# Regrouping layer 1's contractions on one Trainium2 core: two jobs of two per image, with free places ahead of them and behind the projections

## The chip, the cores and the metric

The kernel runs on one core of a Trainium2 chip. That core has a tensor engine (PE in the profile, with PEld for its loads of weights), a vector engine (DVE), a scalar engine (ACT), a GpSimd engine (POOL) and a sync engine (SP), which here does nothing but issue transfers. Each engine works through its own instructions in order and waits on semaphores for the others. Transfers run on 16 DMA engines. The metric is the time of one execution on the device, in microseconds (us); the time of before is the median of three runs.

## The reference: what is computed

The input `x` is 8 images of 56 x 56 pixels with 384 channels, in float32. Two layers of "outlook" attention follow each other, each around a group normalisation and with a residual sum. Cut to layer 1, the one that the change touches:

```python
x = x + conv1(group_norm(x, G=32))          # layer 0 has the same frame around its own conv0

def conv1(x):                               # HEADS = 6, K = 3, head width 64
    a = softmax((x @ W_attn + b_attn).reshape(B, H*W, 6, 9))   # nine weights a pixel and head
    v = x @ W_v + b_v
    patches = stack([pad(v)[:, i:i+H, j:j+W] for i in range(3) for j in range(3)])
    y = einsum('bpKhd,bphK->bphd', patches, a)                 # weighted sum of the 3x3 neighbours
    return y @ W_proj + b_proj
```

Each pixel gets, per head, nine weights from a softmax, takes the weighted sum of the values of its 3x3 neighbours, and is projected. Layer 0 is richer (nine outputs per pixel, which are folded back), and its code is not changed.

## The kernel before

The images are taken in four pairs; a pair's 112 rows lie on the partitions, and the kernel walks over the 56 columns of each pair. Seven columns make a block (`PX = 7`), so each pair has eight blocks and layer 1 has 32, numbered `g`. One step of layer 1's loop (line 1290) is one column.

For each column `attend` (line 1105) projects 128 pixels to the 54 weights and 384 values: three matmuls into one of three PSUM tiles called `bank` (f32 matmuls stand as two records each in the trace, so six). Since 112 rows don't fill 128 partitions, eight columns are packed into seven tiles, and in one step of eight `attend` does nothing ("the attend falls out"). DVE adds the biases; POOL stores the weights into the tile of the block (`at`, kept in `xr_home` and `xin_home`) and the values into a table in DRAM, `vtab`.

When a block's columns are complete, `weigh` and `share` do its softmax on DVE and ACT, and `move` (line 1157) shifts it between rows with three matmuls (`pw` in the trace) and copies it with nine ACT copies into `wz`, which SP sends to one of three tables in DRAM, `ztab`. From there SP loads the block's weights as a banded matrix: `z`, two transfers for each image (`bands`). The values come back as patches, `vp`, one transfer for each image (`fetch_v`): image 0's at step `turn == 5` and image 1's inside `fetch` (line 1195). `z` has three buffers, `vp` has two.

`fetch` then queues the block's jobs on PE. `contract(t)` multiplies a patch row tile: 12 matmuls, 90 rows by 64 columns of the array, into a PSUM tile `pc` of which there are two (`NC = 2`); ACT copies it to `yT`. Each image has four of them, t = 0 to 3, the last of half size: 24, 24, 24 and 12 records. When both images are in `yT`, `project_out(half, j)` (line 1230) does six projections (`po`): three channel groups for the first four columns of the block, three for the other three. DVE adds bias and residual and transposes the result into `ot`; after the third of each half four transfers `out<-ot` are put on the list `later`, which `flush` sends out on SP's queue.

The order of all this is written out by hand. `Jobs` (line 359) is a list of jobs with due steps, and each step of the loop gives it two places: one ahead of `attend` (line 1301) and one behind `attend` and `move` (line 1324). A place takes one job, if the first in the list is due. Seven steps have 14 places. A block's list has seven jobs of contractions (image 0: t = 0 and 1 together, then 2, then 3; image 1: four single ones), one empty job, and six projections: 14. Behind each of the two places stands a `flush`; `fetch`, with its loads of `z` and of image 1's `vp`, stands at the end of the step with `turn == 0`. SP's queue therefore has its transfers in the order in which the loop wrote them.

In the profile all matmuls stand under line 129 and all other operations of layer 1 under line 144, since helpers record them; they are told apart by their tiles. `wv_t` is the home of layer 1's output weights in `po<-yT,wv_t`.

Of the kernel before, what the change touches and what calls it, by code (L numbers as in the profile page):

```python
# [15 lines left out]
def two_outlook_layers(  # L16
# [89 lines left out]
    def by_quadrant(ap, r0, col, n, b):  # L106
        first = r0 * W * C + col * C + b * QC
        return bass.AP(ap.tensor, ap.offset + first, [[W * C, R], [C, n], [1, QC]])
# [19 lines left out]
    def matmul(*args, **kwargs):  # L128
        tc.keep_in_program_order(nc.tensor.matmul(*args, **kwargs))  # L129
# [26 lines left out]
    def projected(name):  # L156
        return patch.tile([P, NCH, PX, IMG, H], F32, tag="yT", name=f"yT_{name}", bufs=1)
# [187 lines left out]
    def bands(queue, z, table, line, slot, row, top, groups, b, py, npy):  # L345

        for (s0, s1), (m0, m1) in groups:
            first = (b * H + top) * line + s0 * slot + m0 * row
            queue.dma_start(
                z[s0:s1, :, m0 * row : m1 * row],  # L350
                bass.AP(
                    table.tensor, table.offset + first + bands.at[row],
                    [[slot, s1 - s0], [py * line, npy], [1, (m1 - m0) * row]],
                ),
            )
# [34 lines left out]
    jobs, norms = Jobs(), Jobs()  # L390
# [26 lines left out]
    def project_half(po, w, yT, half, j):  # L417
        lo, hi = HALVES[half]
        for i in range(NCH):
            matmul(  # L420
                po[:, : (hi - lo) * R],
                w[:, i, j * P : (j + 1) * P],
                yT[:, i, lo:hi].rearrange("p m b y -> p (m b y)"),
                start=(i == 0), stop=(i == NCH - 1),
            )

    def layer0(late, pools):
# [508 lines left out]
        normed(1, SHARED, both=True)  # L936
        LAG = 4
        ahead = layer1((xr_home, xt_homes, xin_home, xn_homes, wa_home, wv_t), late_w)
        last_step = NPAIR * W - 1
        first_of = {last_step - 40: 1, last_step - 7: 1, last_step - 6: 1, last_step - 5: 1}  # L940
# [98 lines left out]
    def layer1(homes, late_w):  # L1039
# [19 lines left out]
        def load(g, queue=sync):  # L1059
            pair, px = divmod(g, NPX)  # L1060

            if g % 5 == 4:
                t = wide(3, lambda size: late_w.tile(size, F32, tag="xres", name="wide_3", bufs=1))
            elif g % 5 == 3:
                t = halves[3]
            elif g % 5 == 2:
                t = wide(2, lambda size: pool.io.tile(size, F32, name="wide_2", bufs=1))
            else:
                t = wide(g % 5, lambda size: (xr_home, wa_home)[g % 5][:, : size[1]])
            t = t[:, : NCH * T].rearrange("p (i t) -> p i t", i=NCH)  # L1070
            queue.dma_start(t, x1s[pair][px])
            x1ts[g] = t.rearrange("p i (m r) -> p i m r", m=PX)
# [117 lines left out]
        def fetch_v(g, b):  # L1190

            vps[g, b] = patch_tiles(f"1_{g}", b)[: SX1 * SY1, :NPY1]
            rows_to_patches(sync, vps[g, b], vtab1, g % NPX, b * H + MARGIN - 1, PY1, NPY1, SX1)

        def fetch(g, due):
            pair, px = divmod(g, NPX)
            n_tile = 2
            yT = projected(f"1_{g}")
            x1t = x1ts.pop(g)
            for b in range(IMG):  # L1200
                bands(
                    sync, zs1[(g * IMG + b) % NZ], ztab1[g % NTAB1], LINE1, SLOT1, ROW1, MARGIN - 1,
                    GROUPS1, b, PY1, NPY1,
                )
            fetch_v(g, 1)
            for b in range(IMG):
                z, vp = zs1[(g * IMG + b) % NZ], vps.pop((g, b))

                def contract(t, b=b, z=z, vp=vp):
                    lo, hi = t * n_tile, min(NPY1, (t + 1) * n_tile)  # L1210
                    pc = ps.tile([P, NCH, n_tile, PY1, PX], F32, tag="c", name=f"pc1_{g}_{b}_{t}", bufs=NC)
                    for py in range(lo, hi):
                        zp = z[:, py].rearrange("s (y h m) -> s y h m", y=PY1, h=HEADS1)
                        for h in range(HEADS1):
                            i, j = divmod(h, P // D1)
                            matmul(
                                pc[j * D1 : (j + 1) * D1, i, py - lo],
                                vp[:, py, h * D1 : (h + 1) * D1],
                                zp[:, :, h, :],
                                start=True, stop=True,  # L1220
                            )
                    scalar.copy(
                        yT[:, :, :, b, lo * PY1 : hi * PY1],
                        pc[:, :, : hi - lo].rearrange("p i n y m -> p i m (n y)"),
                    )

                for ts in ((0, 1), (2,), (3,)) if b == 0 else ((0,), (1,), (2,), (3,)):
                    jobs.add(due, lambda ts=ts, f=contract: [f(t) for t in ts])

            def project_out(half, j):  # L1230
                lo, hi = HALVES[half]
                n = (hi - lo) * R
                po = ps.tile([P, 4 * R], F32, tag="ot"[(half + j) % 2], name=f"po1_{g}_{half}_{j}")
                project_half(po, wo_t, yT, half, j)
                res = x1t[:, j, lo:hi].rearrange("p m r -> p (m r)")
                vector.scalar_tensor_tensor(
                    res, po[:, :n], bo_t[:, j : j + 1], res, ALU.add, ALU.add
                )

                if j == 0:  # L1240
                    fetch.ot = pool.io.tile([P, NR * 4 * QC], F32, tag="ot", name=f"ot_{g}_{half}")
                ot = fetch.ot[:, : NR * (hi - lo) * QC]
                vector.transpose(
                    ot.rearrange("p (s m c) -> p s m c", s=NR, c=QC)[:, :, :, j::NCH],
                    bass.AP(
                        x1t.tensor, x1t.offset + j * T + lo * R,
                        [x1t.ap[0], [1, NR], [R, hi - lo], [NR, Q]],
                    ),
                )
                if j == NCH - 1:  # L1250
                    for b in range(NQ):
                        later.append(
                            lambda b=b: sync.dma_start(
                                by_quadrant(out, pair * R, px * PX + lo, hi - lo, b),
                                ot[b * Q : b * Q + LANES],
                            )
                        )

            if g:
                jobs.add(due, lambda: None)  # L1260
            for half in range(2):
                for j in range(NCH):
                    jobs.add(due, lambda half=half, j=j: project_out(half, j))

        load(0, nc.gpsimd)
        rows_of_channels(wc_t[:, :, :NA1], wa1, nc.gpsimd)
# [23 lines left out]
        for step in range(AHEAD, (NG + 1) * PX + BEHIND):  # L1290
# [41 lines left out]
            if of > 1 and turn == 0:  # L1332
                assert len(cleared) >= min(2 * of - 2, NZ)
                fetch(of - 2, base + step + 3)
            if of == NG and turn == 4:
                fetch_v(NG - 1, 0)
                fetch(NG - 1, base + step + 1)
            elif 0 < of < NG and turn == 5:
                fetch_v(of - 1, 0)
# [49 lines left out]
```

## Time and profile before

| | us |
|---|---|
| three runs | 3172.67, 3184.32, 3172.41 (median 3172.67) |
| the profiled execution | 3169.09 |
| its span | 3166.6, mean granted clock of PE 0.991 |
| layer 1 in full swing, 2300 to 2500: PE busy | 199.55 of 200 |
| the same stretch, DVE / ACT / POOL busy | 100.47 / 48.04 / 80.91 |
| the same stretch, DMA share and rate | 0.96, 237 GB/s |
| start of the first contraction of neighbouring blocks | 2448.88, 2480.99, 2513.10 |

The profile gives each engine's busy time, groups of instructions by line and tile, and a chain of waits: from the last instruction back to what released it, step by step. A line of the chain has its start, its length and what it was, with the number of records. SPq lines are transfers issued by SP: their length is the time that the issuing took, not that of the transfer. "DMA share" is the mean busy share of the 16 DMA engines. Bracketed at the end of a line of the timeline is the idle time ahead of it and what ended it. The layers overlap for a while around 2100 us, where layer 0 ends.

### The profile page before, as it was taken

What the parts mean: (1) busy time and instruction counts of PE and PEld (TensorE: products, weight loads), DVE (VectorE), ACT (ScalarE), POOL (GpSimd) and SP (SyncE); (2) the same over time, 40 slices, a digit from 0 to 9 for tenths busy, and PEclk for the clock granted to TensorE, in tenths of its full rate; (3) what the DMA queues carried; (4) which work ended last, traced back from release to release, by engine and by line L of the source; (5) the groups of instructions that cost most, each with busy time, mean ns of one, the idle gap of its engine ahead of it and who ended that gap; (6) DMA issues with size and microseconds to landing.
All of it is one profiled execution on the core that took longest, in us unless ns stands there. A gap on an engine that the chain in (4) does not pass through costs nothing. (4 is left out here: it accounts for less than half of the span.)

```text
span 3166.6 us, 72796 instructions
## 1 busy us (share of the span) xinstructions
PE 3065.6 (97%) x27640; PEld 2093.9 (66%) x27640; DVE 2079.1 (66%) x4945; ACT 1007.4 (32%) x2426; POOL 1645.7 (52%) x2758
## 2 busy tenths in 40 slices
PE   6899999999999999999999999989999999999998
PEld 5667766777777777776676677645656666565655
DVE  5777777777777777777777677735545454545545
ACT  4333343333333333333333233322222222222221
POOL 2765566565556665666566566643443434344440
PEclk9999999999999999999999999999999999999999
DMA  9799987899998799998889897898999999999997
GB/s 298 223 302 316 321 262 259 297 311 297 311 311 268 255 299 299 318 293 289 274 275 257 291 309 239 259 347 213 231 234 238 240 232 237 237 230 236 234 237 169
DMA packets 619841, 850.84 MB, mean 269 GB/s; under 512 B 264927, under 2 KB 496563, under 8 KB 611171
## 3 DMA queue, kind: packets, MB, share of 16 engines
q1 hardware_dynamic: 554946, 726.37, 76.8%
q0 software_dynamic: 63968, 118.11, 12.3%
q8 instruction: 217, 3.56, 0.5%
q10 hardware_dynamic: 576, 1.72, 0.2%
q14 instruction: 134, 1.09, 0.1%
HBM read 514.86 MB, written 322.17 MB: 264 GB/s over the span
## 5 line engine op out<-in xcount | busy, mean ns | idle before, releaser
L129 PE MATMUL bank<-wa_t,xn 128*128 128x288 f32 x3528 | 971.6, 412 | 16.3 <-ACT xn L144 9.8
L144 POOL TENSOR_TENSOR at<-at,d 128x972 f32<-128x972 f32 x196 | 441.3, 2251 | 713.9 <-DVE d L144 389.0
L129 PEld LDWEIGHTS bank<-wa_t,xn 128*128 128x128 f32 x3528 | 649.9, 191 | 227.4 <-issue 17.6
L144 ACT ACTIVATE at<-at 128x972 f32<-128x972 f32 x196 | 198.7, 1014 | 950.5 <-DVE at L144 950.2
L144 DVE TENSOR_REDUCE mx<-bank 128x36 f32<-128x324 f32 x588 | 284.3, 483 | 315.3 <-PE bank L129 313.5
L129 PE MATMUL bank<-xt,xn 128*128 128x438 f32 x1176 | 477.6, 542 | 2.8 <-ACT xn L144 2.8
L129 PE MATMUL po<-yT,wo_t 128*128 128x336 f32 (+1 forms) x1152 | 417.6, 499 | 15.4 <-DVE x1t L144 14.9
L129 PE MATMUL bank<-wv_t,xn 128*128 128x384 f32 x1176 | 415.7, 490 | 0.0
L129 PEld LDWEIGHTS pc<-z,vp 121*32 121x32 f32 (+1 forms) x17664 | 335.7, 118 | 112.0 <-issue 83.2
L129 PE MATMUL po<-yT,wv_t 128*128 128x336 f32 (+1 forms) x1152 | 394.1, 494 | 2.5 <-ACT yT L144 2.5
L129 PE MATMUL pc<-z,vp 121*32 121x49 f32 (+1 forms) x17664 | 373.2, 217 | 17.1 <-issue 8.6
L144 ACT COPY yT<-pc 128x294 f32<-128x294 f32 (+2 forms) x512 | 206.0, 411 | 428.2 <-PE pc L129 425.2
L129 PEld LDWEIGHTS po<-yT,wv_t 128*128 128x128 f32 x1152 | 218.8, 190 | 170.9 <-issue 123.0
L129 PEld LDWEIGHTS bank<-xt,xn 128*128 128x128 f32 x1176 | 214.5, 190 | 171.9 <-issue 151.8
L129 PEld LDWEIGHTS po<-yT,wo_t 128*128 128x128 f32 x1152 | 214.8, 192 | 147.2 <-issue 75.5
L144 DVE TENSOR_TENSOR at<-bank,mx 128x324 f32<-128x324 f32 x588 | 291.3, 495 | 31.0
L129 PEld LDWEIGHTS bank<-wv_t,xn 128*128 128x128 f32 x1176 | 221.6, 191 | 132.8 <-issue 10.4
L144 POOL DMA_DIRECT2D vtab<-v x476 | 289.4, 612 | 15.3 <-DMA vtab<-zeros 6.4
L144 POOL TENSOR_TENSOR pre<-at,at 112x108 f32<-112x108 f32 (+1 forms) x440 | 236.6, 538 | 76.9 <-DMA at<-at 29.1
L144 DVE TENSOR_TENSOR xt<-bank,ba_t 128x54 f32<-128x54 f32 x147 | 31.1, 212 | 262.9 <-PE bank L129 252.9
L144 ACT ACTIVATE wts<-pre,inside 112x48 f32<-112x48 f32 (+4 forms) x672 | 179.3, 358 | 74.3 <-DMA ztab<-wts 62.6
L1123 POOL DMA_DIRECT2D xin_home<-xt x147 | 76.8, 526 | 212.7 <-DVE xt L144 196.0
(136 smaller groups left out, 3279.9 us busy)
## 6 DMA issues: line engine op xcount, KB each, us to landing
z<-ztab SPq DMA_DIRECT2D x64, 2352.0 KB
vp<-vtab SPq DMA_DIRECT2D x64, 1536.0 KB
vp<-vtab SPq DMA_DIRECT2D x64, 945.0 KB
xres<-xT SPq DMA_DIRECT2D x32, 1176.0 KB
ztab<-wts SPq DMA_DIRECT2D x336, 110.2 KB
xin_home<-xT SPq DMA_DIRECT2D x52, 672.0 KB
xr_home<-in_x SPq DMA_DIRECT2D x50, 672.0 KB
vtab<-v POOLq DMA_DIRECT2D x100, 336.0 KB, 6.7
```

The source lines that it names most:

```text
L129: tc.keep_in_program_order(nc.tensor.matmul(*args, **kwargs))
L144: return lambda *args, **kwargs: tc.keep_in_program_order(op(*args, **kwargs))
L1123: nc.gpsimd.dma_start(at_of(g_of)[row : row + n, m_of].rearrange("r k h -> r (k h)"), lg[lo : lo + n])
```

## The change

Image 0's contractions become two jobs, t = 0 and 1, then t = 2 and 3; image 1's as well. One empty job stands ahead of image 0's first, and two empty jobs stand behind the last projection. The empty job between contractions and projections stays. A block's list is then 1 + 2 + 2 + 1 + 6 + 2 = 14 long, as before.

```diff
-                for ts in ((0, 1), (2,), (3,)) if b == 0 else ((0,), (1,), (2,), (3,)):
+                if b == 0:
+                    jobs.add(due, lambda: None)
+                for ts in ((0, 1), (2, 3)):
                     jobs.add(due, lambda ts=ts, f=contract: [f(t) for t in ts])
...
             for half in range(2):
                 for j in range(NCH):
                     jobs.add(due, lambda half=half, j=j: project_out(half, j))
+            for _ in range(2):
+                jobs.add(due, lambda: None)
```

The orders that result for a block in which no attend falls out, in PE's program order (c0.1 is image 0, t = 1; A an attend; w the move's matmuls; P0 to P5 the projections):

```
before  c0.0 c0.1 c0.2 A w c0.3 c1.0 A c1.1 c1.2 A c1.3 A P0 P1 A P2 P3 A P4 P5 A
after   c0.0 c0.1 A w c0.2 c0.3 c1.0 c1.1 A c1.2 c1.3 A P0 P1 A P2 P3 A P4 P5 A A
```

and of SP's queue, in a block that also loads `x` (the residual of a later block):

```
before  ztab  x  vp(image 0)  z x4  vp(image 1)  out x4  out x4
after   ztab  x  vp(image 0)  out x4  z x4  vp(image 1)  out x4
```

Engines' instructions are the same in number and kind. POOL's order is the same.

## The prediction

> **What bounds the kernel now.** I read the page first, then the busy time by stage, then the chain that ended last inside layer 1, then SP's timeline there.
>
> ```profile
> PE 3065.6 (97%) x27640; PEld 2093.9 (66%) x27640; DVE 2079.1 (66%) x4945; ACT 1007.4 (32%) x2426; POOL 1645.7 (52%) x2758
> ```
>
> ```profile
> 2481.00:2513.00 32.00, 32.00 (x246) 19.35 (x246) 15.50 (x30) 8.24 (x24) 12.77 (x24) 1.00 1.01 253
> ```
>
> The second is one 32 us block of seven columns of layer 1 (columns: length; PE, PEld, DVE, ACT, POOL busy; granted clock; DMA share; GB/s). Two things are full at once: PE has no idle time, and the DMA share is 1.01. The chain of the same block:
>
> ```profile
> 2480.99 2.35 PE pc L129 x72
> 2483.34 2.40 PE bank L129 x6
> 2485.74 0.66 PE pw L129 x6
> 2486.40 1.19 PE pc L129 x36
> 2487.59 2.40 PE bank L129 x6
> 2489.99 1.54 PE pc L129 x48
> 2491.54 2.40 PE bank L129 x6
> 2493.94 0.49 PE pc L129 x12
> 2494.43 2.40 PE bank L129 x6
> 2496.84 4.51 PE po L129 x12
> 2501.35 2.21 PE bank L129 x6
> ```
>
> Four runs of contractions (pc), with an attend (bank) between them, then the six projections (po; the last four, with an attend falling out among them, run from 2503.55 to 2510.89). An attend takes 2.40 us behind a pc run and 2.21 behind po: 0.19 us is the change of weights. Runs of 12, 36 and 48 records take 0.49, 1.19 and 1.54 us, so a run costs 0.14 us plus 29.2 ns a record. SP's queue beside it:
>
> ```profile
> 2487.45 0.31 SPq L144 DMA_DIRECT2D ztab<-wz  x1
> 2487.82 0.57 SPq L144 DMA_DIRECT2D wide<-x  x1
> 2488.61 2.15 SPq L144 DMA_DIRECT2D vp<-vtab  x1
> 2493.97 4.61 SPq L144 DMA_DIRECT2D z<-ztab  x4
> 2498.69 0.49 SPq L144 DMA_DIRECT2D vp<-vtab  x1
> 2507.70 7.75 SPq L144 DMA_DIRECT2D out<-ot  x5
> ```
>
> With S the start of a block's first contraction (2480.99), the next block's z are issued at S+13.0, the second vp at S+17.7, the output of the first half (out0) at S+26.7. The next block contracts from S+32.1. So z and vp have 14 to 19 us to land, and what SP waits for longest, the transposed output, comes behind them.
>
> **The change part by part.** The empty places emit nothing: cost 0 by themselves. What they do is shift jobs by whole places against the attends and against the DMA issues.
>
> *PE.* A block's runs become 48 (image 0, first two), attend, pw, 84 (image 0, last two, and image 1, first two), attend, 36. One run fewer saves 0.14+0.19 = 0.33 us. The 72 run of before had 0.11 us of waiting in it (2.35 against 0.14+72x29.2 ns), which goes. New: in the 84 run the third contraction needs the PSUM buffer of the first, whose ACT copy stands behind the nine wz copies. The trace has that run in the blocks where an attend falls out:
>
> ```profile
> 2357.20 0.67 PE pw L129 x6
> ...
> 2359.10 1.61 PE pc L129 x48
> ```
>
> From pw's end, 2357.87, to the run's end, 2360.71: 2.84 us instead of 2.59. Its first copy was the short one (0.30 us); now it is one of 0.44, so 2.95. Per block: 1.54+2.95+1.19 = 5.68 against 5.57, less 0.19 for one attend: -0.1 us. Bounds: -0.44 (no wait) to +0.2. In the 4 blocks where the attend ahead of pw falls out, the two norm activations of 1.79 us stand ahead of those copies as well: some +1.4 each, between 0 and 1.8. Sum over 29 blocks: -3+6, about nothing. POOL's order is unchanged; DVE and ACT get the same work; DVE is half idle (15.5 of 32 us).
>
> *SP.* This is what decides. The projections come two places earlier: the third (the last of the first half) is now ahead of the block's z loads in program order. So SP's order becomes out0 (4 DMAs), z (4), vp, out1 (4), ztab, x, vp, where it was z, vp, out0, out1, ztab, x, vp. SP issues in order, and out0 waits for DVE's transposes. Behind it now wait z and the second vp of the next block, and out1, ztab, x and vp behind those; for z and vp waits PE. Call T0 the moment out0 is issued.
>
> From the start of image 1's contractions (in the 84 run) to T0: two contractions 1.54, attend 2.40, run of 36 1.19, attend 2.40, two projections 4.51, attend 2.21, third projection 2.24 (half of two); then DVE's add 0.68 and transpose 1.11 and 0.06 of gaps. 16.5+1.85 = 18.35 us.
>
> From T0 to image 1's contractions of the next block: out0's four issues of 0.82 to 0.87 us in the last blocks, then z's first packet 0.8 us behind its issue: 4.4 to 5.4, I take 5.0. The packets of z (840 bytes) and of vp (1536 bytes) are seen in the trace: at the very end, with no stores of POOL beside them, z and vp took 9.9 us (3132.3 to 3142.2); in a full block 14.3 (2468.5 to 2482.8, with up to 1.5 us of neighbours in it). Three attends' stores still fall in the new place, fewer than in a full block since PE will wait: I take 12.6, nearer to the full block. Landing: 1.1 to 1.3 us from the last packet to the end of the wait at 3143.55, in the chain
>
> ```profile
> 3129.84 13.71 DMA vp<-vtab
> ```
>
> So 5.0+12.6+1.2 = 18.8 us, between 15.4 and 21.0. The contractions of image 1 would otherwise start 15.6 us after T0 (third projection over at -1.85; then 1.68+2.21+3.39+2.21+2.21, 1.54+2.40+0.66+1.19), or 13.3 where an attend falls out on the way: PE waits 3.2 to 5.5 us in each block.
>
> The loop closes: 18.35+18.8 = 37.15 us a block, and 34.85 in the 3 blocks of 8 where an attend falls out of the first part; mean 36.3. Before, eight blocks took 2448.88-2189.72 = 259.16 us, 32.4 each. +3.9 us, over 29 blocks +113. The waits on ACT above lie ahead of this wait and are swallowed by it. DMA loses its full load: SP holds everything until T0, and the last load of the round is over about 4 us earlier.
>
> *Clock.* The trace shows what a gap on PE costs behind it:
>
> ```profile
> 2115.34 4.17 PE L129 MATMUL bank<-xt,xn 128*128 128x438 f32 x6 [2.79 <-ACT xn L144]
> 2133.27 4.02 PE L129 MATMUL po<-yT,wo_t 128*128 128x448 f32 x6 [0.49 <-ACT yT L144]
> ```
>
> An attend of 2.40 us took 4.17 behind a gap of 2.79; the projection of 2.24 took 4.02 just behind a gap of 3.42 us. Both had a granted clock of 0.5 for 3.41 us. That is 1.77 us on the path per gap, between 0 and 1.77. Some gaps will be split, a short wait for image 0's z ahead of the longer one; I take four blocks in five: 29x0.8x1.77 = 41.
>
> The Trainium skill ("TensorE: Matmul & The Clock Gate", Part 1) has the clock halve only after an idle window of about 3.4 us. Here 2.79 us were enough, so the row is used; by the rule, only the longer half of the gaps would cost, an estimate of +26 in place of +41, 3312 in all.
>
> Sum: +113+41 = +154. The profiled execution took 3169.09 us (span 3166.6 and 2.5 around it), 0.1% under the median of 3172.67; the change is put on the median: 3327 us.
>
> **Rivals.**
> 1. *The loads are quick* (chance 0.20): z and vp move as at the end, 9.9 us, and the delay is 15.4 to 17 us. The loop is 33.75/31.45 to 35.35/33.05, mean 32.9 to 34.5, +15 to +61, and gaps of 0 to 2 us that may or may not halve the clock (0 to 41): 3188 to 3270. For it: the queue is empty at T0. Against: POOL's stores of three attends are still there.
> 2. *Covered, not slower* (0.08): the one mechanism is that z and vp land within 13.3 us of T0, so that PE never waits and only the PE part counts: 3172 to 3176. The point from which it decides is a delay of 13.3 (15.6 in a full block). Against: 4.4+9.9+1.1 = 15.4 with every term at its least. Faster by more than 0.5% would need over 16 us, and the PE part at its best (-0.44 in 29 blocks) gives 13.
> 3. *DMA pays more* (0.07): 21.0 us of delay and every gap at half clock: 39.35/37.05, mean 38.5, +177+51 = 3400, and more if vp of image 0 still runs at T0, which the lower bound of the idle stretch (4 us a block) speaks against.
>
> **How the numbers follow.** The main case has 0.65, 3270 to 3390 by a delay of 17.3 to 20.5 us. With the larger part of rival 1, 3205 to 3395 holds 8 in 10. Slower by over 0.5%, about what can be told from no change here: 0.65+0.07+0.20, 0.92; within it: 0.06; faster: 0.02, for a gain on PE beyond my bounds; both are rival 2.
>
> **What would show it.** Right: in layer 1, PE waits on vp<-vtab ahead of image 1's contractions, 3 to 5 us in most blocks; the DMA share falls from 1.0 to about 0.88; blocks of 35 to 39 us; SP's out0 of four issues directly ahead of z; attends or contractions behind the gap stretched, clock under 1. Layer 0 (up to some 2100 us) unchanged. Wrong: blocks of 32 us, no wait of PE on a DMA, then the loads were covered. If PE waits on ACT's yT instead, the 84 run was mis-sized.

## The result, and the profile after

The changed kernel takes 3295.53 us (median of 6 runs, 3286.79 to 3311.33) where the kernel before takes 3173.15 (6 runs): 1.0384 times as long, 95% interval 1.0365 to 1.0403, or +122 us. The execution that was profiled is the longest of the six: 3311.33 us with a span of 3309.5, 143 us over the span before. So the trace shows some 16 us more than the median.

Busy times, from the page of the changed kernel:

```profile
span 3309.5 us, 72855 instructions
PE 3116.6 (94%) x27640; PEld 2128.8 (64%) x27640; DVE 2084.9 (63%) x4945; ACT 1004.2 (30%) x2426; POOL 1644.6 (50%) x2758
```

The same 27640 matmul records keep PE busy for 3116.6 us instead of 3065.6, 51 us more. The rest of the 143 us is waiting. Who waited for whom, PE alone, from 2000 us to the end (in total, times, longest):

```profile
PE pc L129 <- DMA vp<-vtab: 48.6, 24, 4.3
PE pc L129 <- DMA z<-ztab: 42.6, 25, 6.4
```

Before, PE waited 1.6 us on vp and not at all on z. 91 us of waiting and 51 of slower work make up nearly all of the 143. The 400 us from 2300 to 2700, with the columns of the stage lines shown above (length; PE, PEld, DVE, ACT, POOL busy; granted clock; DMA share; GB/s), first of the changed kernel:

```profile
2300.00:2700.00 400.00, 366.45 (x2707) 223.99 (x2707) 182.12 (x319) 85.75 (x254) 140.81 (x267) 0.95 0.86 208
```

and of the kernel before:

```profile
2300.00:2700.00 400.00, 399.10 (x2994) 241.08 (x2993) 203.63 (x360) 95.52 (x278) 160.33 (x304) 1.00 0.96 235
```

PE had work without a break and now idles for 34 us of 400, the clock is no longer whole, and the transfers run at 208 GB/s instead of 235 although PE waits for them. Why they do is seen in SP's queue, changed kernel:

```profile
2510.59 3.48 SPq L144 DMA_DIRECT2D out<-ot  x4
2514.17 2.11 SPq L144 DMA_DIRECT2D z<-ztab  x4
2516.45 0.33 SPq L144 DMA_DIRECT2D vp<-vtab  x1
2516.87 6.83 SPq L144 DMA_DIRECT2D out<-ot  x4
2525.71 0.32 SPq L144 DMA_DIRECT2D ztab<-wz  x1
2526.08 3.28 SPq L144 DMA_DIRECT2D wide<-x  x1
2529.59 0.34 SPq L144 DMA_DIRECT2D vp<-vtab  x1
2549.06 3.47 SPq L144 DMA_DIRECT2D out<-ot  x4
```

From the vp issued at 2529.59 to the out at 2549.06 SP issues nothing for 19 us: its next instruction waits for DVE's transposes. The trace has the queue's packets running dry at about 2542 and starting again at 2550. Then z and vp leave at once, and PE wants them. The chain that ended last, changed kernel, over one round:

```profile
2492.11 1.61 PE pc L129 x48
2493.72 2.40 PE bank L129 x6
2496.13 1.19 PE pc L129 x36
2497.32 2.40 PE bank L129 x6
2499.72 4.51 PE po L129 x12
2504.24 2.21 PE bank L129 x6
2506.44 2.27 PE po L129 x6
...
2508.74 0.69 DVE wide L144
...
2509.45 1.04 DVE ot L144
...
2516.45 12.43 DMA vp<-vtab
...
2529.01 2.40 PE pc L129 x48
2531.41 3.19 PE bank L129 x6
```

This is the loop of the prediction, closed: image 1's contractions to the third projection, DVE's add and transpose, out0's issues, z and vp, image 1's contractions again. In some rounds it is z that ends the wait: the next time round the chain goes through `DMA z<-ztab` (5.42 us from 2553.22) to image 0's contractions. The chain is no longer PE alone: over the page's whole span PE has 19% of it and DMA 10%, where it was 31% and 1%. The last two lines show the fallen clock: the two contractions take 2.40 us instead of 1.61, the attend 3.19 instead of 2.40.

### The profile page after: what moved, and what is told of

Same layout as the page of the kernel before. It is cut to its first block, busy times and chain, and to the rows that moved or that the text cites. A ratio compares the mean times of both kernels' runs of the same rounds, so it can differ in the third digit from the quotient of the medians.

```text
span 3309.5 us, 72855 instructions
## 1 busy us (share of the span) xinstructions
PE 3116.6 (94%) x27640; PEld 2128.8 (64%) x27640; DVE 2084.9 (63%) x4945; ACT 1004.2 (30%) x2426; POOL 1644.6 (50%) x2758
## 5 line engine op out<-in xcount | busy, mean ns | idle before, releaser
L129 PE MATMUL bank<-wa_t,xn 128*128 128x288 f32 x3528 | 971.6, 412 | 16.7 <-ACT xn L144 11.5
L129 PE MATMUL bank<-xt,xn 128*128 128x438 f32 x1176 | 502.0, 568 | 4.2 <-ACT xn L144 4.2
L129 PE MATMUL pc<-z,vp 121*32 121x49 f32 (+1 forms) x17664 | 388.9, 220 | 107.2 <-DMA vp<-vtab 48.6
L129 PEld LDWEIGHTS pc<-z,vp 121*32 121x32 f32 (+1 forms) x17664 | 353.1, 122 | 190.1 <-issue 134.8
L129 PEld LDWEIGHTS bank<-xt,xn 128*128 128x128 f32 x1176 | 230.0, 202 | 196.9 <-issue 175.3
L1123 POOL DMA_DIRECT2D xr_home<-xt x147 | 76.8, 526 | 270.9 <-DVE xt L144 247.1
```

The source lines that it names most:

```text
L1123: nc.gpsimd.dma_start(at_of(g_of)[row : row + n, m_of].rearrange("r k h -> r (k h)"), lg[lo : lo + n])
```

## The experiments

Each ratio is against the kernel before on the same chip; the first four runs shared one chip and the last four another.

### The loads put back ahead of the output

```diff
+            loads_first = of > 1 and turn == 0
+            if not loads_first:
-            flush()
+                flush()
             store()
...
                 fetch(of - 2, base + step + 3)
+                flush()
```

> The changed kernel with one thing put back: SP issues the next block's z and image 1's vp ahead of out0, as before; PE's new grouping stays. Theory L (the cost is SP holding z and vp behind out0): 3165 to 3182 us, what the PE part alone was priced at (-0.1 us a block, some +1.4 in four blocks), no wait of PE on vp or z in layer 1, DMA share back at 0.95. Rival P (the cost is the new grouping itself, its waits on ACT's copies): still 3270 or more, with PE waiting on yT copies. Rival C (a clock that falls for another reason): still half-clock stretches in layer 1.

Measured: 3186.81 us, ratio 1.0040 (1.0025 to 1.0055). Nearly all of the loss is gone with PE's grouping unchanged. PE's waits in layer 1, this run:

```profile
PE pc L129 <- ACT yT L144: 11.4, 30, 1.4
PE bank L129 <- ACT xn L144: 6.3, 9, 3.4
PE pc L129 <- DMA vp<-vtab: 4.1, 1, 4.1
PE pc L129 <- DMA z<-ztab: 1.7, 1, 1.7
```

One wait each on vp and z is left, both in the last blocks (3143.0 and 3149.8). The DMA share is back at 0.95 (2300 to 2700). So the order of the loads accounts for some 110 of the 122 us, and the grouping itself is not free: +13 us (0.4%), outside the 3165 to 3182 that I had given. The trace of this run, whose span is 10.5 us over that of before, shows where it goes. The 24 blocks between the third and the 27th out0 take 32.8 us each instead of 32.4, 9.5 us together: PE waits there 9.1 us for ACT's copies (0.2 us in most blocks, 1.4 in one of eight, not more than priced) and 2.2 us for norms (not priced), and behind two of the waits of 1.4 us the clock falls. The last stretch, from the 27th out0 to the end, takes 149.6 us instead of 140.6 (not priced either), and the first out0 comes 8 us earlier than before. What makes PE wait on ACT is that, with the projections done early, two attends follow each other ahead of the contractions, so that the softmax (DVE), its Exp and the norms (ACT) no longer have the time of two projections to get out of the way. The chain of this run at one such place:

```profile
2509.94 0.27 ACT xr_home L144
2510.21 0.15 issue
2510.37 0.56 ACT xn L144
2510.93 0.14 issue
2511.07 0.79 ACT xn L144
2511.86 0.66 ACT yT L144 x2
2512.51 2.25 ACT xn L144 x4
2514.76 0.87 ACT wz L144 x9
2515.63 0.31 ACT yT L144
```

Exp (xr_home), norms (xn) and copies stand in one row on ACT, with 0.15 us between them at most, and PE is at the end of it.

### The old grouping with the loads behind the output

```diff
-            if of > 1 and turn == 0:
+            if of > 1 and turn == 1:
                 assert len(cleared) >= min(2 * of - 2, NZ)
-                fetch(of - 2, base + step + 3)
+                fetch(of - 2, base + step + 2)
```

> The kernel before with the old grouping, but z and image 1's vp issued one step later, behind out0. Theory L: from image 1's contractions to out0 the old order takes 0.70+2.40+1.54+2.40+0.49+2.40+4.51+2.21+2.24+1.85 = 20.7 us, then 18.5 to the loads' landing: 39.2, less 2.3 in half of the blocks, mean 38.1 against 32.4: +165, and up to 40 for the clock: 3310 to 3390, more than the change itself. Rival P: 3173, since the grouping is the old one.

Measured: 3357.72 us, ratio 1.0576 (1.0558 to 1.0594), inside the range. PE's waits, from 2150 us:

```profile
PE pc L129 <- DMA z<-ztab: 84.5, 30, 6.1
PE pc L129 <- DMA vp<-vtab: 27.8, 12, 4.8
```

The kernel before, with nothing changed but the place of five transfers in SP's queue, loses more than the changed kernel does, since out0 comes later in its block (over 24 rounds 20.5 us on average behind the start of image 1's contractions, 18.9 in the changed kernel). From the issues of out0, 24 blocks average 38.5 us, the fallen clock included, against 38.1 worked out without it. With the run above this settles it from both sides: the order on SP is needed for the loss, and is enough for it.

### Only part of the loads behind the output

With z ahead and vp behind, the `flush` stands between the two in `fetch`:

```diff
+            flush()
             fetch_v(g, 1)
```

> The changed kernel with z put ahead of out0 and only image 1's vp left behind it. Theory L by its terms: 3.6 us of out0's issues, 1.0 to the first packet, vp's 5 us with 1.5 of POOL's stores, 1.2 of landing, 12 to 13 us behind out0, under the 13.3 to 15.6 after which PE wants it: covered, 3168 to 3190. If any load behind out0 makes PE wait: 3240 or more.

Measured: 3192.88 us, ratio 1.0056 (1.0038 to 1.0074). That is just over the range given, and 6 us over the run with all loads ahead, a difference within the two intervals. In layer 1 no wait of PE is put down to either transfer (one of 5.7 us in the last block has no releaser in the trace); the rest is the grouping's own price. 3.48 us of issues and one vp behind out0 fit into what PE has to do.

With vp ahead and z behind:

```diff
+            fetch_v(g, 1)
+            flush()
             for b in range(IMG):
                 bands(
...
-            fetch_v(g, 1)
```

> The changed kernel with image 1's vp put ahead of out0 and z left behind it. Theory L by its terms: z's four transfers land 5.0+6.4+1.5+1.2 = 14 us behind out0, 0 to 0.8 over what image 1 leaves; image 0's pair lands at about 9.9, and PE wants it at 7.7 in the blocks with an attend less, at 9.9 in the others: waits of 0.5 to 2 us on z in most blocks, none on vp, 3200 to 3260. If only the sum of what stands behind out0 counted, it would be near the run with vp behind (z is 1034 KB, vp 945): 3193.

Measured: 3250.62 us, ratio 1.0243 (1.0214 to 1.0272), inside the range. PE's waits, from 2150 us:

```profile
PE pc L129 <- DMA z<-ztab: 47.2, 28, 6.9
PE pc L129 <- ACT yT L144: 9.5, 30, 1.4
```

Two loads of nearly the same size, 1034 and 945 KB, cost some 64 us and at most a few in the same place, against the run with all loads ahead. What counts here is not how much stands behind the waiting output but when PE wants it: z is wanted by image 0 already.

### Work in the gap

Six matmuls of 336 columns ahead of image 1's first contraction, written into the PSUM tile that the contraction then overwrites:

```diff
+                    if b == 1 and t == 0 and 0 < g < NG - 1:
+                        for _ in range(6):
+                            matmul(
+                                pc.rearrange("p i n y m -> p (i n y m)"), wo_t[:, 0, :P],
+                                wo_t[:, 1, : NCH * n_tile * PY1 * PX], start=True, stop=True,
+                            )
```

> The changed kernel with six matmuls of 336 columns (some 3.4 us of PE work, written into the PSUM tile of image 1's first contraction, which overwrites it) ahead of that contraction in 30 blocks, so that PE works through most of the gap in which it waits for vp. If the fallen clock behind the gap is on the path (PE's busy time grew by 51 us): fewer half-clock stretches than the 131 us that layer 1 gained, and 3240 to 3290. If the fallen clock costs nothing: 3295, or up to 30 more where the gap is shorter than the filler.

Measured: 3342.91 us, ratio 1.0532 (1.0514 to 1.0550): a miss, 47 us slower than the changed kernel. The clock did recover (0.984 against 0.970), but PE hardly waited on vp any more (0.2 us) while it still waited 44.3 us on z: part of the gap lies ahead of image 0, and the filler, 3.8 us a block, was longer than what is left of it ahead of image 1. The run says nothing on the clock's price. So a shorter one, two matmuls ahead of each image (`t == 0`, `range(2)`):

> The changed kernel with two matmuls of 336 columns (1.1 us) ahead of image 0's first contraction and two ahead of image 1's, in 30 blocks, written into the PSUM tile that the contraction overwrites. The long filler was longer than the gap, which the wait on z had already shortened; this one fits. If the fallen clock is on the path: gaps mostly under 1 us, half-clock stretches in layer 1 well under the 137 us of the changed kernel, and 3255 to 3290 us. If it is not: 3293 or more.

Measured: 3284.09 us, ratio 1.0340 (1.0315 to 1.0364), inside the range and just clear of the changed kernel's interval. The mean granted clock is 0.987. A clock that is either whole or half gives 2 x (1 - clock) x span of half rate: with the clock unrounded, 57 us before, 196 in the changed kernel, 88 here. The matmuls put in are busy for 82 us, and the waits that remain do not shrink by as much (from 91 us to some 33 from 2150 us on, ACT's included); yet the run is 11 us faster by the medians. Adding 82 us of PE work makes this kernel faster: the fallen clock is on the path. How much of it, the two traces show where PE works without a wait on loads, from image 1's contractions to out0. Over the same 24 rounds that way takes 18.88 us on average in the changed kernel, where half-rate stretches fall into 13 of them, and 17.67 here, where they fall into none. So the fallen clock costs some 1.2 us a block on the path; the half rate that falls ahead of image 1's contractions is mostly swallowed by the wait for vp.

### The projections left where they were

The same jobs, two of two per image, with the free places moved: none ahead, four between contractions and projections, none behind.

```diff
-                if b == 0:
-                    jobs.add(due, lambda: None)
                 for ts in ((0, 1), (2, 3)):
...
-            if g:
+            for _ in range(4 if g else 3):
                 jobs.add(due, lambda: None)
...
-            for _ in range(2):
-                jobs.add(due, lambda: None)
```

> The changed kernel's two jobs of two for each image, but with the free places put elsewhere: none ahead of the contractions, four between them and the projections, none behind. Projections and SP's order are then those of before. PE: two runs of 84 instead of four runs. Theory L: no wait of PE on vp or z, and only the PE part: 2.70+2.95 = 5.65 us of contractions against 5.57, two attends at 2.21 instead of 2.40, -0.3 a block, +1.35 in the four blocks where the norm stands ahead of the copies, about -4 in all: 3165 to 3180, ratio 0.997 to 1.002. Rival P: the grouping costs by itself, 3187 or more.

Measured: 3160.17 us, ratio 0.9953 (0.9935 to 0.9970): faster than both kernels, and 0.5% faster than the kernel before. The chain, one block:

```profile
2508.16 2.70 PE pc L129 x84
2510.86 2.40 PE bank L129 x6
2513.27 0.65 PE pw L129 x6
2513.92 2.65 PE pc L129 x84
2516.57 6.82 PE bank L129 x18
2523.39 4.51 PE po L129 x12
2527.90 2.21 PE bank L129 x6
2530.11 3.95 PE po L129 x12
2534.06 2.21 PE bank L129 x6
2536.26 3.39 PE po L129 x12
```

Two runs of contractions instead of four, the projections and SP's order as before, a block of 31.5 us instead of 32.1. The second run takes 2.65 us, not the 2.95 that I expected: its first two contractions are both of full size and last until ACT has got through the wz copies, whereas in the changed kernel the short t = 3 stands among them, and PE waits 0.2 us there in most blocks of the first experiment's trace and not at all in most blocks of this one. That is most of why the gain is 0.5% rather than the tenth of a per cent of my estimate.

With image 1's first two copies on DVE and the norm one step later as well:

```diff
-                    scalar.copy(
+                    (vector.tensor_copy if b and t < 2 else scalar.copy)(
...
-            if m == 0 and 0 < g < NG:
+            if m == 1 and 0 < g < NG:
                 normed(g, 3, PX)
```

> The same as the run with the projections in their old places, with the two things moved that stand in the way of the second run of 84: image 1's first two copies of contractions go to DVE, which is half idle, and the norm of a block's last four columns is issued one step later. If ACT's queue is what the longer runs wait for: 5.3 us of contractions, -0.27-0.38 = -0.65 us a block, 3152 to 3165, ratio 0.993 to 0.998. If DVE's copies get in the way of its evictions for the attends: 3173 or more.

Measured: 3162.13 us, ratio 0.9955 (0.9937 to 0.9973), the same as without. In the run before there was next to no wait on ACT left to remove (2.9 us in 4 places), so here neither the engine of the copies nor the place of the norm matters.

## Why the prediction was right, point by point

- **What decides is SP's order.** Right, and shown from both sides by the first two experiments.
- **From image 1's contractions to out0, 18.35 us.** 2492.11 to 2510.59 is 18.48, and so are all full blocks at full clock; it is 20.05 where the clock had fallen (2529.01 to 2549.06). The sum counts an attend behind a run of contractions 0.19 us longer than one behind a projection, and the chains agree (2.40 and 2.21); that the 0.19 us is a change of weights no run shows.
- **From out0 to image 1's contractions, 18.8 us.** Too long by 1.1. 2510.59 to 2529.01 is 18.42, but over 24 rounds it is 17.7 on average (16.3 to 19.3): 5.1 from out0 to the first packet of z, 11.5 for the packets of z and vp, 1.1 from there to PE's start, where 5.0, 12.6 and 1.2 were added up. The mis-sized term is the packets: 11.5 us lies between the two stretches that the estimate was taken from (9.9 and 14.3), nearer to the one without POOL's stores.
- **The block: 36.3 us, and 1.4 for the clock.** The issues of out0 that frame 24 blocks lie at 2261.1 and 3138.6: 36.56 each, against 32.40 before. The loop was right; its way from out0 was 1.1 us too long, and that is what puts the block 1.1 us under the 37.7 forecast (36.3 and 1.4). The clock term was about right, 1.2 us a block against 1.4. About every second wait falls on image 0's z, and where the clock falls there, the slow work behind it lies ahead of the wait for vp and is mostly swallowed by it.
- **The tail was not priced.** The last blocks have no attends and took 27 and 20 us before; they now take 34 as well. From the 27th out0 to the end the trace has 171 us against 141. It hides in part that the blocks cost less than forecast: of the profiled run's +143, the 24 blocks make 100, where the forecast has 127, and the rest 43, where it has 27. That the profiled run comes within 11 us of the forecast +154 is in part luck, since the two errors cancel; the median, +122, is 16 us under the profiled run, and why the other runs are shorter (clocks of 0.972 to 0.975 against 0.970) was not traced.
- **PE's part, about nothing.** Too low: +13 us by the first experiment. The waits for copies were no larger than priced (11.4 us in all). Not priced were the waits for norms, the clock that falls behind the longest of these waits, and the longer last blocks; with the first out0 coming 8 us earlier, that run's trace shows +10.5 us in all. In the changed kernel PE's waits on copies are 1.4 us in all: as forecast, the wait on the loads swallows them.
- **DMA share down to about 0.88, a wait of PE on vp of 3 to 5 us.** The share is 0.86. The wait on vp was 2 us on average and at most 4.3, because z took nearly as much again ahead of it; in that size the forecast was wrong.
- **The rivals.** "Covered" is what happens when only vp stands behind the output, and "loads are quick" did not occur as a whole, though 4 of the 24 rounds have a delay of 17.0 us or less.

## What to carry to other kernels

A job that is moved on one engine takes its transfers with it. Where one queue issues everything in order, look at what a moved job's output is now ahead of, and at what that output waits for: five loads behind one waiting store cost 3.4% here (1.0384 against 1.0040), with the store itself no larger. Grouping the same work was worth 0.5% as soon as the free places were put where the queue's order stayed what it was.

## What the runs showed that was not expected

The clock of PE halves after gaps far shorter than the 2.79 us that the prediction used, and not after each of them. From 2150 us on, the changed kernel's trace has 39 gaps of PE of over 1 us and 23 stretches at half rate, most of 3.4 or 6.8 us. Such stretches begin within 0.5 to 1.3 us of the end of gaps of 1.38, 1.69, 2.2 and 3.17 us, while gaps of 1.23, 1.66, 2.3 and 2.88 us are followed by none within 9 us. So the length of a single gap is no sure sign either way. What tells more is where the gaps lie: the starts of all 23 stretches lie whole multiples of 3.413 us apart, on one grid. Of the grid's intervals at full clock from 2160 us on, each of the 10 in which PE idles for more than 1.8 us in all is followed by half rate, none of those with less than 1.3 us is, and 12 of the 17 in between are. The rule of an idle window of about 3.4 us (the Trainium skill, "TensorE: Matmul & The Clock Gate", Part 1), by which I had put the clock's cost at 26 us in place of 41, does not describe these gaps if the whole window has to be idle: halvings behind gaps of 1.38 to 2.2 us are none that it then allows for. Its smaller sum, 3312 us, came nearer to the measured time, but by luck, since the clock cost some 1.2 us a block, nearer to the 1.4 of the forecast, and it was the loads that took less.

Nor had I expected that matmuls of no use could pay for themselves: 82 us of them, with the clock at 0.987 in place of 0.970, made the changed kernel 11 us faster by the medians, and a longer filler in the same gap made it 47 us slower.
